# Layer 1 of a four-image kernel: TensorE's order made by an account of the engines instead of a fixed rate

## The chip, the cores and the metric

One core of a Trainium2 chip runs the whole program. The metric is the device time of one execution in microseconds (us). No die comparison is possible with one core; every run quoted here is of the undisturbed state ("fast"), and where single executions scatter, the granted TensorE clock of the record is given beside them.

## The reference, cut to what matters

Input x is 4 x 256 x 48 x 48, float32. Layer 0 is a normalised 3x3 convolution followed by attention over 2304 positions; layer 1 computes 45 guidance channels, turns them into weights by softmax, sums nine weighted shifts of the image for each of five dilations, and mixes the six results with a 1x1 convolution.

```python
def _L1_conv_ref(x, W_cat, W_scale, gamma, beta):          # cut
    guidance = _conv(x, W_cat, pad=1)                       # 45 channels
    outs = [x]
    for i, d in enumerate((1, 6, 12, 24, 36)):
        w = softmax(guidance[:, 9*i:9*(i+1)], axis=1)
        outs.append(_dyn_branch(x, w, d))                   # sum of 9 shifted, weighted copies
    y = _conv(concatenate(outs, axis=1), W_scale, pad=0)
    ...                                                     # batch normalisation over all images
# x = x + layer0(group_norm(x)); x = x + layer1(group_norm(x))
```

## The kernel before

Layer 1 of an image goes in six chunks of 384 positions. For each shift (a "tap") TensorE broadcasts the tap's weights over the partitions with one matmul into PSUM (`wb`), VectorE multiplies them with the shifted image (`prod`, or `cat` for the first tap of a dilation), and GpSimd adds the product to `cat`. When a dilation is complete, TensorE mixes it into `py` with four matmuls. Names of tiles in the profiles: the guidance goes `pg`, `lg`, `pt` (transposed), `e` (softmax), `pw` (transposed back), `w` (the weights); the convolution goes `pc`, then `cs` and `yt` (output transform), `hid`; `pq` and `pv` are the q, k and v products, `se` and `p` the scores and exponentials of the attention. In the trace of this kernel TensorE starts nothing of what stands behind a waiting matmul in its order: before the `pw` at 732.25 us, which waits for `w`, it stands 7.24 us without a matmul, and the filler behind it starts only at 732.94 us. So the program has to put other TensorE work between the `wb` matmuls: mixes that are due, steps of the next guidance (`ahead`), and the next image's convolution and q, k, v products (`other`, the filler). Before, a constant rate per element decides how much:

```python
            rate = (max(left, 0.0) + GUIDE * (NCK // 2 - 1) * 2 / NCK + mixes) / TAP_ELEMENTS
            ...
            def pump():
                nonlocal owed
                while owed > 0:
                    if queue and queue[0][0] <= tap:            # a mix, due so many taps later
                        owed -= queue.pop(0)[1]()
                        continue
                    if pace[1] < pace[0]:                       # a step of the next guidance
                        ...
                    got = next(other, None)                     # filler
                    ...
                    owed -= got
            ...
                    single = alone and at > 0 and j >= 10 and j % 5 == 0
                    ...                                         # wb matmul, product
                    if single:
                        ...                                     # TensorE mixes this product itself
                    elif at:
                        nc.gpsimd.tensor_tensor(dst, dst, pv, ALU.add)
                    tap += 1
                    owed += NH * nr * ncol * rate
                    pump()
            ...
            run(1e9)                                            # what is left of the filler
            for _, go in queue:                                 # then the last mixes
                go()
```

`alone` is the last image, which has no filler; there some taps are "single": TensorE mixes the product and GpSimd has no add. The convolution that serves as filler ends in an output transform on VectorE. Four of its instructions per unit (an image has four units) read two operands from SBUF (`d34` with `d12`, `s34` with `s12`):

```python
                elif i == 4:
                    tt(s34, m, first[at], ALU.add)              # m is in PSUM
                    tt(d34, first[at], m, ALU.subtract)
                elif i == 0:
                    result(1, d34, -2.0, d12)                   # yt <- cs, cs: both in SBUF
                    result(2, s34, -4.0, s12)
                    tt(s12, s12, s34, ALU.subtract)
                    axpy(d12, d34, -8.0, d12)
                    result(0, m, None, s12)
```

## Time and profile before

In profile lines PE is TensorE, PEld its weight loads, DVE VectorE, ACT ScalarE, POOL GpSimd and SPq a DMA queue; `a<-b` names what is written and what is read, and L with a number is a line of the kernel.

| | before |
|---|---|
| time, median of 3 runs | 3043.45 us (3041.85 to 3043.84) |
| span of the profiled execution | 3038.6 us |
| GpSimd's adds in the first layer-1 stage | 192, 258.6 us |
| TensorE's waits in it (six kinds) | 26.0 us |
| granted clock of TensorE, 545 to 868, 1262 to 1594 and 1985 to 2322 us | 0.98, 0.97, 0.97 |
| the same, 644.5 to 647.9, 709.3 to 712.7 and 729.8 to 736.6 us (13.6 us of the first stage) | 0.50, 0.51, 0.50 |
| the same, 720 to 740 us, which hold the 7.24 us wait of `pw` | 0.83 |
| first `wb` of the stage to the first exponential of the next attention | 301.9, 302.1, 302.1 us |

The prediction below shows the page, the groups and the waits of this kernel. Two more readings of it turn out to matter. First, the two `yt<-cs` groups of VectorE in the table of groups: in the window 545 to 868 us (the first layer-1 stage, with GpSimd adding) and in the window 0 to 140 us (the first image's own convolution, with GpSimd idle). The number after the comma is the mean of one instruction in ns.

```profile
L755 DVE SCALAR_TENSOR_TENSOR yt<-cs 128x288 f32<-128x288 f32 x8 | 9.3, 1199 | 0.0
...
L755 DVE SCALAR_TENSOR_TENSOR yt<-cs 128x288 f32<-128x288 f32 x8 | 3.3, 448 | 0.3 <-ACT hid L742 0.3
```

The same eight instructions on the same shapes take 1199 ns beside GpSimd's adds and 448 ns without them. The prediction used 1.2 us as if it were the work of the instruction.

Second, the end of the first stage in the timeline (start, duration, engine, and in brackets the idle time before it and what ended it): the last mixes, the copy of y, its store, and the first exponential of the attention that follows.

```profile
860.92 5.41 PE L1189 MATMUL py<-cat,wsc 128*128 128x384 f32 x16
...
866.41 0.80 ACT L1207 COPY y<-py 128x768 f32<-128x768 f32 x1 [4.84 <-PE py L1189]
867.23 0.51 SPq L1211 DMA_DIRECT2D y_d<-y  x1
...
870.52 3.77 ACT L906 ACTIVATE p<-se 128x1024 f32<-128x1024 f32 x4 [3.32 <-DMA y_d<-y]
```

The exponentials wait 3.3 us for the store of y, and TensorE, which has issued its first scores, waits behind them.

### The profile page before, as it was taken

What the parts mean: (1) busy time and instruction counts of PE and PEld (TensorE: products, weight loads), DVE (VectorE), ACT (ScalarE), POOL (GpSimd) and SP (SyncE); (2) the same over time, 40 slices, a digit from 0 to 9 for tenths busy, and PEclk for the clock granted to TensorE, in tenths of its full rate; (3) what the DMA queues carried; (4) which work ended last, traced back from release to release, by engine and by line L of the source; (5) the groups of instructions that cost most, each with busy time, mean ns of one, the idle gap of its engine ahead of it and who ended that gap; (6) DMA issues with size and microseconds to landing.
All of it is one profiled execution on the core that took longest, in us unless ns stands there. A gap on an engine that the chain in (4) does not pass through costs nothing. (4 is left out here: it accounts for less than half of the span.)

```text
span 3038.6 us, 43039 instructions
## 1 busy us (share of the span) xinstructions
PE 2836.5 (93%) x17526; PEld 1312.7 (43%) x17526; DVE 2425.0 (80%) x2312; ACT 1549.2 (51%) x1812; POOL 1107.0 (36%) x833
## 2 busy tenths in 40 slices
PE   7999999998999999998899999999899999987984
PEld 5622224565642222565662222346564222244653
DVE  6399999578869999777868999967776999976776
ACT  3489888101258888500218988820124888850003
POOL 1000000997930000488880000079794000006884
PEclk9999999999999999999999999999999999998997
DMA  4400000011030000010003000000002000022004
GB/s 175 94 1 6 6 11 7 27 36 34 19 79 6 6 1 11 22 42 24 29 6 79 6 6 11 6 27 27 21 6 42 6 1 6 11 88 90 1 1 178
DMA packets 77966, 95.54 MB, mean 31 GB/s; under 512 B 52144, under 2 KB 66752, under 8 KB 75968
## 3 DMA queue, kind: packets, MB, share of 16 engines
q1 hardware_dynamic: 76960, 87.31, 10.0%
q0 software_dynamic: 800, 5.41, 0.5%
q8 instruction: 139, 2.28, 0.3%
q14 instruction: 67, 0.55, 0.1%
HBM read 62.03 MB, written 30.67 MB: 31 GB/s over the span
## 5 line engine op out<-in xcount | busy, mean ns | idle before, releaser
L906 ACT ACTIVATE p<-se 128x1024 f32<-128x1024 f32 x1296 | 1259.3, 1026 | 252.2 <-PE se L897 215.9
L944 DVE TENSOR_TENSOR acc<-acc,p 128x2048 f32<-128x2048 f32 x536 | 1227.9, 2291 | 75.7 <-ACT p L906 29.5
L1280 POOL TENSOR_TENSOR cat<-cat,prod 128x752 f32<-128x752 f32 (+7 forms) x734 | 992.6, 1361 | 570.3 <-DVE prod L1267 529.5
L897 PE MATMUL se<-q,k 32*128 32x512 f32 (+1 forms) x5760 | 805.4, 593 | 12.4 <-ACT p L906 7.5
L1267 DVE TENSOR_TENSOR prod<-wb,pad 128x768 f32<-128x768 f32 (+7 forms) x768 | 552.5, 747 | 203.5 <-PE wb L1243 165.2
L927 PE MATMUL num<-p,vT 128*32 128x512 f32 (+1 forms) x5760 | 694.8, 562 | 8.6 <-ACT scratch L949 7.4
L897 PEld LDWEIGHTS se<-q,k 32*128 32x128 f32 x5760 | 292.6, 183 | 529.5 <-issue 307.9
L714 POOL TENSOR_TENSOR cv_q<-pad,cv_q 128x600 f32<-128x600 f32 x3 | 4.1, 1354 | 1317.3 <-ACT cv_q L712 1317.3
L1243 PE MATMUL wb<-w,pick 128*128 128x384 f32 (+3 forms) x888 | 434.3, 524 | 21.9 <-DVE prod L1267 21.3
L1189 PE MATMUL py<-cat,wsc 128*128 128x384 f32 x960 | 364.8, 506 | 29.0 <-POOL cat L1280 28.9
L927 PEld LDWEIGHTS num<-p,vT 128*32 128x32 f32 x5760 | 121.8, 108 | 487.5 <-issue 439.8
L1189 PEld LDWEIGHTS py<-cat,wsc 128*128 128x128 f32 x960 | 182.9, 197 | 126.3 <-POOL cat L1280 36.2
L1243 PEld LDWEIGHTS wb<-w,pick 128*128 128x128 f32 x888 | 167.1, 193 | 140.0 <-DVE prod L1267 43.4
L810 PE MATMUL pc<-cv_q,u 128*128 128x288 f32 x576 | 168.2, 424 | 6.3 <-DVE cv_q L716 6.3
L810 PE MATMUL pc<-cv_k,u 128*128 128x288 f32 x576 | 159.3, 406 | 1.4 <-ACT m L767 1.2
L1067 PE MATMUL pg<-pad,wcat 128*45 128x384 f32 x864 | 153.7, 499 | 2.4 <-DVE pad L589 1.5
L1260 DVE TENSOR_TENSOR cat<-wb,pad 128x768 f32<-128x768 f32 x120 | 114.2, 952 | 41.6 <-PE wb L1243 41.4
L742 ACT ACTIVATE hid<-yt,bn_t_f,bn_s 128x288 f32<-128x288 f32 x64 | 39.4, 625 | 199.6 <-DVE yt L755 114.1
L838 PE MATMUL pq<-hid,wqkv 128*128 128x384 f32 x384 | 135.7, 485 | 0.0
L810 PEld LDWEIGHTS pc<-cv_q,u 128*128 128x128 f32 x576 | 110.7, 199 | 32.6 <-DVE cv_q L716 6.3
L810 PEld LDWEIGHTS pc<-cv_k,u 128*128 128x128 f32 x576 | 105.8, 189 | 27.8 <-issue 1.8
L944 DVE TENSOR_TENSOR acc<-p,p 128x2048 f32<-128x2048 f32 x36 | 82.5, 2292 | 41.8 <-ACT p L906 41.8
(209 smaller groups left out, 1631.2 us busy)
## 6 DMA issues: line engine op xcount, KB each, us to landing
pad<-in_x SPq DMA_DIRECT2D x14, 1152.0 KB, 14.9
u<-u_d SPq DMA_DIRECT2D x18, 768.0 KB, 4.3
x_d<-pad SPq DMA_DIRECT2D x48, 192.0 KB, 2.5
xst<-in_x SPq DMA_DIRECT2D x36, 192.0 KB, 2.4
y_d<-y SPq DMA_DIRECT2D x18, 384.0 KB, 2.7
u_d<-u SPq DMA_DIRECT2D x6, 768.0 KB, 3.8
y<-y_d SPq DMA_DIRECT2D x2, 2304.0 KB, 14.2
x<-x_d SPq DMA_DIRECT2D x2, 2304.0 KB, 21.5
```

Of the source, the lines that this page charges most:

```text
L810: nc.tensor.matmul(m, u[:, h, kx, o * P : (o + 1) * P], halves[g][:, h, i, :, kx : kx + WW], start=(h == 0 and kx == 0), stop=(h == NH - 1 ...
L838: nc.tensor.matmul(pq[:, :CH], wqkv[:, i, s, g * P : (g + 1) * P], hid[:, i, cols], start=(i == 0), stop=(i == NH - 1),)
L897: nc.tensor.matmul(ss[j // 2][:, j % 2, at : at + n], k_[r, g, m * P : (m + 1) * P], q[r, g, q0 : q0 + n], start=True, stop=True,)
L906: nc.scalar.activation(p[:, 2 * pair : 2 * pair + 2, :], ss[pair], AF.Exp, scale=QS)
L927: nc.tensor.matmul(st["num"][r, at : at + n], vT[:, m, g * P + j * D : g * P + (j + 1) * D], p[:, j, at : at + n], start=(m == 0 and not s ...
L944: nc.vector.tensor_tensor(st["acc"], other, p, ALU.add)
L1067: nc.tensor.matmul(pg[64 * s : 64 * s + NG, :CH], wcat[:, i, k, :], window(gn, i, (c + s) * R, k // 3 - 1, k % 3 - 1), start=(i == 0 and k ...
L1189: nc.tensor.matmul(to, wsc[:, n * NH + i, o * P : (o + 1) * P], rhs(i), start=(n == 0 and i == 0), stop=(last and i == NH - 1),)
L1243: nc.tensor.matmul(pw[:, : nr * WW], pick[:, k : k + 1].to_broadcast([P, P]), w[:, l0 * WW : l1 * WW], start=True, stop=True,)
L1260: nc.vector.tensor_tensor(catv, wb, src, ALU.mult)
L1267: nc.vector.tensor_tensor(pv, wb, src, ALU.mult)
L1280: nc.gpsimd.tensor_tensor(dst, dst, pv, ALU.add)
```

## The change

Its intent: give TensorE other work exactly as long as the next `wb` would have to wait for its buffer. The program keeps, while it is being built, an account of when each engine is expected to be done (`Clock`), with a fixed duration for each instruction. Other work is issued until TensorE's account reaches the time at which the buffer comes free; a mix goes out when its addend is expected to be ready. In the last image a tap is single when GpSimd's account is further behind than TensorE's by `BEHIND`. At the end of a stage the queued mixes now come first and the rest of the filler last. A check of a flag in the last image also moves one chunk later.

```diff
+        class Clock:
+            def __call__(self, engine, ns, *after):
+                self.t[engine] = max(self.t[engine], *(a + 150.0 for a in after), 0.0) + ns
+                return self.t[engine]
...
                     else:
                         axpy(t, x, a, y)
+                        end = clock("DVE", 1200)
... (some thirty such entries)
-            def pump():
-                nonlocal owed
-                while owed > 0:
-                    if queue and queue[0][0] <= tap:
-                        owed -= queue.pop(0)[1]()
+            def fill(until):
+                while clock.t["PE"] < until:
+                    if queue and when(queue[0]) <= clock.t["PE"]:
+                        queue.pop(0)[-1]()
                         continue
... (then guidance steps, then filler, as before)
+                    fill(slot("wb", 5 if alone else 3))
                     pw = ps_w.tile([P, 512], F32, tag="w", name=f"wb_{b}_{c}_{k}")
...
-                    single = alone and at > 0 and j >= 10 and j % 5 == 0
+                    single = (
+                        alone and at > 0
+                        and clock.t["POOL"] + added > clock.t["PE"] + len(queue) * NH * MM + BEHIND
+                    )
...
+            while queue:
+                fill(when(queue[0]))
+                if queue:
+                    queue.pop(0)[-1]()
             ...
             run(1e9)
-            for _, go in queue:
-                go()
```

More of the change, by code (lines that the diff above doesn't have):

```diff
@@ L38 @@
 PRODS = 5
+BEHIND = 4000.0
 CONV_B, BN_G, BN_B, BN_M, BN_V, Q_B, K_B, PROJ_B, G1, B1 = range(10)
@@ L636, in conv_preact_kernel, with __init__, level, slot @@
         MM = 27.0 / 16 * CH
+        class Clock:
+            def __init__(self):
+                self.t = dict.fromkeys(("PE", "DVE", "ACT", "POOL"), 0.0)
+            def __call__(self, engine, ns, *after):
+                self.t[engine] = max(self.t[engine], *(a + 150.0 for a in after), 0.0) + ns
+                return self.t[engine]
+            def level(self):
+                self.t = dict.fromkeys(self.t, max(self.t.values()))
+        clock = Clock()
+        free = {}
+        def slot(tag, bufs):
+            ends = free.setdefault(tag, [])
+            return ends[-bufs] if len(ends) >= bufs else 0.0
         ORDER = (1, 2, 3, 4, 0, 5)
@@ L760, in result @@
                         tt(t, x, y, ALU.add)
+                        end = clock("DVE", 450, clock.t["PE"])
                     else:
                         axpy(t, x, a, y)
+                        end = clock("DVE", 1200)
                     relu(g, o, r, t)
+                    clock("ACT", 630, end)
+                    return end
                 if i in (1, 3):
@@ L767, in outputs @@
                     nc.scalar.copy(first[at], m)
+                    end = clock("ACT", 400, clock.t["PE"])
                 elif i == 2:
@@ L770, in outputs @@
                     tt(d12, first[at], m, ALU.subtract)
+                    end = clock("DVE", 900, clock.t["PE"])
                 elif i == 4:
@@ L773, in outputs @@
                     tt(d34, first[at], m, ALU.subtract)
+                    end = clock("DVE", 900, clock.t["PE"])
                 elif i == 0:
@@ L778, in outputs @@
                     axpy(d12, d34, -8.0, d12)
-                    result(0, m, None, s12)
-                else:
-                    result(3, m, None, d12)
+                    clock("DVE", 1400)
+                    end = result(0, m, None, s12)
+                else:
+                    end = result(3, m, None, d12)
+                free["c"].append(end)
             if b == 0:
@@ L807, in conv @@
                         m = pc[:, :TN]
+                        clock("PE", 0, slot("c", 2))
                         for h in range(NH):
@@ L816, in conv @@
                                 )
+                                clock("PE", MM * TN / CH)
                                 if h < NH - 1 or kx < 2:
@@ L836, in conv_qkv @@
                         pq = psum_tile(f"pq_{b}_{c}_{g}_{s}")
+                        end = clock("PE", 2 * MM, slot("c", 2))
                         for i in range(NH):
@@ L847, in conv_qkv @@
                         )
+                        free["c"].append(clock("ACT", 580, end))
+                        clock("DVE", 550, clock.t["ACT"])
                         nc.vector.tensor_reduce(
@@ L864, in conv_qkv @@
                 nc.scalar.copy(vT[:, t : t + 2, :], pv)
+                end = clock("PE", 4 * MM * C / CH, slot("c", 2))
+                free["c"].append(clock("ACT", 590, end))
                 if t == 0:
@@ L874, in conv_preact_kernel @@
         qkv = {}
-        CONV_QKV = MM * (6 * 4 * 6 * TN / CH + NCK * NH * 4 + NT * 2 * C / CH)
         def attention(b, q, k_, vT, pools, spare, project, scratch):
@@ L1074, in weights @@
                         if k % 3 == 2:
+                            clock("PE", 3 * MM)
                             yield 3 * MM
@@ L1077, in weights @@
                 nc.vector.tensor_copy(lg[64 : 64 + NG, :], pg[64 : 64 + NG, :CH])
+                clock("ACT", 480, clock.t["PE"])
+                clock("DVE", 560, clock.t["PE"])
                 yield -300.0
@@ L1095, in weights @@
                 nc.vector.tensor_reduce(mx, lt, AX.X, ALU.max)
+                clock("PE", 600)
+                clock("DVE", 430, clock.t["PE"])
                 yield -600.0
                 nc.vector.tensor_tensor(ek, lt, each(mx), ALU.subtract)
+                clock("DVE", 430)
                 yield -600.0
@@ L1102, in weights @@
                 nc.vector.tensor_reduce(sm, ek, AX.X, ALU.add)
+                clock("DVE", 430)
                 yield -600.0
                 nc.vector.reciprocal(sm, sm)
+                clock("DVE", 330)
                 yield -600.0
@@ L1107, in weights @@
                 nc.vector.tensor_tensor(ek, ek, each(sm), ALU.mult)
+                clock("DVE", 1800)
                 for _ in range(3):
@@ L1125, in weights @@
                     out.append(w)
+                    clock("PE", 600)
+                    clock("ACT", 480, clock.t["PE"])
+                    clock("DVE", 560, clock.t["ACT"])
                     yield -500.0
@@ L1131, in dynamic_filters @@
             ready = {}
-            GUIDE = 2 * NCK // 2 * 9 * MM
             while chunk < NCK:
@@ L1151, in dynamic_filters, with when, waiting, mixed @@
                     run(-got)
-            mixes = NCK * (1 + len(DILATIONS)) * NH * NH * MM
-            left = (CONV_QKV - spent[0] - 9000.0) if other is not None else 0.0
-            rate = (max(left, 0.0) + GUIDE * (NCK // 2 - 1) * 2 / NCK + mixes) / TAP_ELEMENTS
             queue = []
-            tap = 0
-            owed = 0.0
             ahead = iter(())
-            def pump():
-                nonlocal owed
-                while owed > 0:
-                    if queue and queue[0][0] <= tap:
-                        owed -= queue.pop(0)[1]()
-                        continue
-                    if pace[1] < pace[0]:
-                        got = next(ahead, None)
-                        if got is not None:
-                            pace[1] += 1
-                            owed -= max(got, 0.0)
-                            continue
-                    got = next(other, None)
-                    if got is None:
-                        owed = 0.0
-                        return
-                    owed -= got
+            def when(entry):
+                return entry[0] if entry[1] else slot("y", 1) + 150
+            def fill(until):
+                while clock.t["PE"] < until:
+                    if queue and when(queue[0]) <= clock.t["PE"]:
+                        queue.pop(0)[-1]()
+                        continue
+                    if pace[1] < pace[0] and next(ahead, None) is not None:
+                        pace[1] += 1
+                        continue
+                    if next(other, None) is None:
+                        return
+            def waiting(kind):
+                return sum(entry[1] == kind for entry in queue)
+            def mixed(kind, most):
+                while waiting(kind) > most:
+                    fill(when(queue[0]))
+                    if queue:
+                        queue.pop(0)[-1]()
             def mix(c, n, o, rhs, last=False, at=None):
@@ L1195, in go @@
                         )
+                    part = 1.0 if at is None else (l1 - l0) * (x1 - x0) / CH
+                    clock("PE", NH * MM * part, slot("y", 1) if n == 0 and o == 0 else 0.0)
                     if last and o == NH - 1:
                         done(c)
-                    return NH * MM
                 return go
@@ L1207, in done @@
                 nc.scalar.copy(yc, py.pop(c)[:, :, :CH])
+                free["y"].append(clock("ACT", 800, clock.t["PE"]))
+                clock("DVE", 1100, free["y"][-1])
                 for o in range(NH):
@@ L1215, in dynamic_filters @@
             STEPS = 24.0
+            clock.level()
+            free.update((tag, []) for tag in ("wb", "prod", "y"))
             for c in range(NCK):
@@ L1218, in dynamic_filters @@
                     back()
+                if alone and c == 2:
                     flag_of(misc("pf")[:1, : B * NH])
@@ L1224, in dynamic_filters @@
                     queue.append(
-                        (
-                            tap + (9 if alone else 14),
-                            mix(c, 0, o, lambda i, c=c: window(gn, i, c * R, 0, 0)),
-                        )
+                        (0.0, "", mix(c, 0, o, lambda i, c=c: window(gn, i, c * R, 0, 0)))
                     )
@@ L1235, in dynamic_filters @@
                     if at == 0:
+                        mixed("cat", NH * (CATS - 1))
                         cat = work1.tile(
@@ L1256, in dynamic_filters @@
                     src = gn[:, :, 1 + y0 + oy : 1 + y1 + oy, 1 + x0 + ox : 1 + x1 + ox]
-                    single = alone and at > 0 and j >= 10 and j % 5 == 0
+                    clock("PE", 0.45 * nr * WW + 20, slot("wb", 5 if alone else 3))
+                    ns = NH * nr * ncol
+                    ns, added = 1.05 * ns + 150, 2.1 * ns + (190 if ncol == WW else 80)
+                    single = (
+                        alone and at > 0
+                        and clock.t["POOL"] + added > clock.t["PE"] + len(queue) * NH * MM + BEHIND
+                    )
                     if at == 0:
                         nc.vector.tensor_tensor(catv, wb, src, ALU.mult)
+                        end = summed = clock("DVE", ns, clock.t["PE"])
                     else:
+                        if single:
+                            mixed("single", 2 * NH)
                         tag, bufs = ("single", 3) if single else ("prod", PRODS)
@@ L1267, in dynamic_filters @@
                         nc.vector.tensor_tensor(pv, wb, src, ALU.mult)
+                        end = clock(
+                            "DVE", ns, clock.t["PE"], 0.0 if single else slot("prod", PRODS)
+                        )
+                    free["wb"].append(end)
                     if single:
@@ L1270, in dynamic_filters @@
                             queue.append((
-                                tap + 6,
+                                end + 150, "single",
                                 mix(
@@ L1280, in dynamic_filters @@
                         nc.gpsimd.tensor_tensor(dst, dst, pv, ALU.add)
-                    tap += 1
-                    owed += NH * nr * ncol * rate
+                        summed = clock("POOL", added, end)
+                        free["prod"].append(summed)
                     pace[0] += STEPS * 1.15 * NH * nr * ncol * NCK / 2 / TAP_ELEMENTS
-                    pump()
                     if j + 1 == len(taps) or taps[j + 1][0] != n:
                         for o in range(NH):
-                            queue.append(
-                                (
-                                    tap + PRODS + 1,
-                                    mix(
-                                        c, n + 1, o, lambda i, cat=cat: cat[:, i, :],
-                                        n == len(DILATIONS) - 1,
-                                    ),
-                                )
-                            )
+                            queue.append((
+                                summed + 150, "cat",
+                                mix(
+                                    c, n + 1, o, lambda i, cat=cat: cat[:, i, :],
+                                    n == len(DILATIONS) - 1,
+                                ),
+                            ))
                 if c % 2 == 1:
@@ L1298, in dynamic_filters @@
                         pass
+            while queue:
+                fill(when(queue[0]))
+                if queue:
+                    queue.pop(0)[-1]()
             if alone:
```

## The prediction

> **What bounds the kernel now.** I read the page first (busy shares and the 40 slices), then the groups, the waits and the timeline of single stretches. The program takes four images in turn, each an attention stage and then a layer-1 stage; layer 1 of images 0 to 2 carries the convolution of the next image along as filler for TensorE, the last image has no filler.
>
> ```profile
> PE 2836.5 (93%) x17526; PEld 1312.7 (43%) x17526; DVE 2425.0 (80%) x2312; ACT 1549.2 (51%) x1812; POOL 1107.0 (36%) x833
> PE   7999999998999999998899999999899999987984
> POOL 1000000997930000488880000079794000006884
> ```
>
> GpSimd works in layer 1 alone: 545 to 868, 1262 to 1594, 1985 to 2322 and 2712 to 3004 us, some 1280 us in all. The change rearranges nothing outside these; the attention stages (about 1610 us) stay. The groups of image 0's layer 1, 545 to 868 us:
>
> ```profile
> L1280 POOL TENSOR_TENSOR cat<-cat,prod 128x768 f32<-128x768 f32 (+9 forms) x192 | 258.6, 1356 | 34.9 <-DVE prod L1267 24.0 <-POOL cat L1280 0.3
> L1267 DVE TENSOR_TENSOR prod<-wb,pad 128x768 f32<-128x768 f32 (+9 forms) x192 | 138.7, 746 | 48.1 <-PE wb L1243 36.4 <-POOL cat L1280 10.8
> ```
>
> GpSimd's 192 adds take 258.6 us, and stand between 572.6 and 861.8 us (289 us): it is 89% busy. To compare, I count TensorE's stream[...]. In the timeline a group of four py records (two matmuls of 384 columns) and one wb repeat every 1.47 us, so a matmul is 0.64 us and a wb 0.19. From the first wb on the stage issues py 144 x 0.64 = 92, wb 41, conv and q, k, v about 105, guidance 23, small ones 4: some 263 us in 301. So both are near full, and **GpSimd is the tighter one**. The waits of the same stage:
>
> ```profile
> PE pw L1114 <- DVE w L1122: 7.4, 2, 7.2
> PE py L1189 <- POOL cat L1280: 7.3, 6, 2.7
> PE wb L1243 <- DVE prod L1267: 7.1, 8, 3.0
> POOL cat L1280 <- DVE prod L1267: 24.0, 14, 4.2
> ```
>
> TensorE waits some 25 us per stage, but what ends the stage is GpSimd, and its reachable loss is the 24.0 us it waits for products; the other 10.9 of 34.9 us are about 55 ns at each of 192 adds and stay. Fourteen of the 24 us lie between 690 and 745 us. There:
>
> ```profile
> 695.49 3.06 DVE L755 SCALAR_TENSOR_TENSOR yt<-cs 128x288 f32<-128x288 f32 x2
> 700.58 7.53 POOL L1280 TENSOR_TENSOR cat<-cat,prod 128x576 f32<-128x576 f32 x5 [2.35 <-DVE prod L1267]
> ...
> 704.68 2.58 DVE L755 SCALAR_TENSOR_TENSOR yt<-cs 128x288 f32<-128x288 f32 x2
> ```
>
> VectorE, not TensorE, is overfull: the convolution's four result units (from the table of groups, two of 1.2 us, one of 0.96, two of 0.45 each, some 4.3 us per unit) stand in front of the products.
>
> In the last image (158 adds, 216.4 us) GpSimd waits 457.3 - 435.7 = 21.6 us for products. The longest piece is the chain that makes the tap weights, with nothing beside it:
>
> ```profile
> 2887.24 2.14 PE L1067 MATMUL pg<-pad,wcat 128*45 128x384 f32 x12
> ...
> 2895.27 0.88 PE L1114 MATMUL pw<-ident,e 128*128 128x128 f32 x3 [3.36 <-DVE e L1107]
> ...
> 2900.35 3.06 POOL L1280 TENSOR_TENSOR cat<-cat,prod 128x672 f32<-128x672 f32 x2 [7.17 <-DVE prod L1267]
> ```
>
> [...]1005 ns for 384 elements, 1820 for 768, a slope of 2.12 ns. The new account uses 2.1 ns plus 80 or 190, so its GpSimd is right to about 1% (1803 against 1820; 1659 against 1653 for 752 elements). Its VectorE (1.05 ns plus 150: 956 against 950) is right too. [...]the 7.2 us wait of pw held all filler behind it. [...]the 20 us that hold this wait show a granted clock of 0.83.
>
> **The change part by part.** I compared the built orders; counts of work are unchanged in images 0 to 2.
>
> (a) *The account instead of a rate, images 0 to 2.* Before each wb, TensorE is given other work only until the wb's buffer is expected free. In the built order the work ahead of the 60th wb falls from 68 to 61 us, of the 120th from 138 to 134, of the 216th from 245 to 239; the adds up to there need 73, 144 and 256. So products run ahead of GpSimd more, and the waits outside the crowded stretch (24.0 - 14.0 = 10 us) should shrink to about 3, the 1 to 2 us of the start among them: gain 7.
>
> (b) *The crowded stretch.* The new order still feeds the four result units within about 14 taps. There VectorE needs 4 x 4.3 = 17 for the units, 4 for statistics and weights, 13 for the products: 34 us. GpSimd needs 20 us for those adds and holds at most five products, about 7 us. It must idle about 34 - 20 - 7 = 7 us where it lost 14. Gain 7, the least certain term.
>
> (c) *The end of the stage.* Before, all v matmuls were issued before the last mixes. Now four pv groups (4 x 1.7 = 6.8 us) stand after them. In the old trace the last mixes streamed until 866.4 and the next exponentials waited until 870.5 for the store of y; that is 8.7 us after the last add. In the new order it is 2.6 (last mix) + 6.8 + 1.5 = 10.9, but the store is then hidden. Loss 2.
>
> Per image 7 + 7 - 2 = 12; I take 11, since three timings must hold together. Three images: 33 us.
>
> (d) *The last image.* Singles fall from 34 to 25 but become larger ones. By the per-form durations GpSimd's adds rise from 218 to 222 us, TensorE's single mixes fall from 58 to 54: nearly no transfer of load. Against that, the account has less reason to fill, so the guidance steps lag: the built order now has two bare chains. After the last wb of chunk 1 come two guidance steps, the transposes and both pw before the first wb of chunk 2; the same at chunk 3 to 4 with one step. From the old trace, last pg to next wb is 2889.4 to 2897.9, 8.5 us. With 3.9 us of pg ahead and 2.3 us to the first new add, less about 4 us of held products, GpSimd idles some 10.7 us; for the second chain 1.9 + 8.5 + 2.3 - 3.5 = 9. Two chains cost 20 where one cost 7.2. The remaining 14 us of waits should fall to about 6. Net: 4 + 13 - 8 = 9 us longer; I take 8, as the account might use the pause.
>
> Sum: -33 + 8 = -25 us, 3043 - 25 = **3018 us**.
>
> **The rivals.** *TensorE is the bound, and its waits (25 to 28 us per stage, plus some 7 us of slow clock) all come back.* For it: 93% busy and a busy map of nines. Against: streaming only 263 of 301 us, and GpSimd's 258.6 us of adds with 10.9 us of gaps start at 572.6, so they cannot end before 842. Even with every wait gone this gives 20 us per image: about 2980 with a neutral last image. *The bare chains dominate.* If both cost 15 us and the crowded stretch does not improve, the sum is 3 x -4 + 18: about 3050. *The account is off at each step because it doesn't know the statistics and normalisation of VectorE (12 x 0.55 us per stage)*, so wb matmuls wait for buffers in order[...]. Then the gain of (a) vanishes and (c) stays: about 3043 to 3055. The durations agree so well that I give this little weight.
>
> **Range and chances.** Terms (a) and (b) together may be 4 to 19 us per image, (d) may be -6 to +20: 3018 less 32 at best and plus 25 otherwise. Range 2986 to 3043. Over 2% faster means below 2982.6, which needs nearly all of GpSimd's waits back in all four images: 0.08. Over 2% slower (above 3104) would need a stall that I don't see in the order: 0.02. Within 2%: 0.90.
>
> **What would show it.** (a): GpSimd's wait for products per stage falls from 24 to about 10 us, adds still 258.6. (b): what remains sits where VectorE runs the STT results. (c): pv matmuls after the last py, and no wait of the exponentials for y's store. (d): in the last image two GpSimd waits of 8 to 11 us, each behind the weights' chain, and about 167 adds of 222 us. The prediction is wrong if adds themselves get longer, if the wait of wb for products grows, or if the two chains are covered.

## The result, and the profile after

The changed kernel took 3027.09 us (median of 4 runs, 3026.57 to 3028.31) against 3043.44 us (median of 4, 3041.85 to 3043.84) of the kernel before. The ratio is 0.9948, 95% interval 0.9931 to 0.9965: the same within 2%, and 16 us faster. Ratios here are the mean time of one kernel's fast runs over that of the other's in the same rounds, so they are not quite the ratio of the medians quoted.

The page of the changed kernel, the same two rows that the prediction shows of before:

```profile
PE 2834.9 (94%) x17454; PEld 1303.8 (43%) x17454; DVE 2419.1 (80%) x2312; ACT 1549.8 (51%) x1812; POOL 1109.4 (37%) x842
...
POOL 1000000898930000389880000078894000007884
```

Busy shares say nothing about the 16 us. The groups of GpSimd in the first stage and its wait, and the waits of TensorE there (total us, times, longest):

```profile
L1349 POOL TENSOR_TENSOR cat<-cat,prod 128x768 f32<-128x768 f32 (+9 forms) x192 | 258.2, 1355 | 29.1 <-DVE prod L1332 18.3
```

```profile
PE pt L1124 <- DVE lg L1117: 6.8, 2, 3.5
PE pw L1162 <- DVE e L1154: 6.2, 2, 6.0
PE pc L844 <- DVE yt L784: 4.2, 2, 2.4
PE pq L874 <- DVE yt L784: 2.0, 1, 2.0
PE wb L1299 <- DVE prod L1332: 1.5, 5, 0.6
PE pw L1162 <- DVE w L1170: 1.2, 2, 1.0
PE py L1240 <- POOL cat L1349: 1.0, 2, 0.7
```

The three waits that led before (pw for w 7.4, py for cat 7.3, wb for prod 7.1) have shrunk to 1.2, 1.0 and 1.5 us: the account does what it was built for. But pt for lg, pw for e, and pc and pq for yt have grown from 3.3 us together to 19.2. The sum is 22.9 us where it was 25.1 for the same kinds. All the new waits stand behind VectorE. The `e` that pw waits for is one of the instructions that run long beside GpSimd, and the `yt` that pc and pq wait for, 0.45 us of work itself, stands behind two more of them in VectorE's order. `lg` is none of them:

```profile
L779 DVE SCALAR_TENSOR_TENSOR yt<-cs 128x288 f32<-128x288 f32 x8 | 9.8, 1259 | 0.0
L1154 DVE TENSOR_TENSOR e<-e,sm 128x270 f32<-128x270 f32 x3 | 4.4, 1478 | 0.1
L1153 DVE TENSOR_TENSOR e<-e,sm 128x270 f32<-128x270 f32 x3 | 3.6, 1194 | 0.0
```

The end of the first stage in the timeline of the changed kernel: the rest of the filler (pv) stands after the last mixes, the store of y lies beside it, and the exponentials wait only for their scores.

```profile
859.83 7.07 PE L895 MATMUL pv<-wqkv,hid 128*128 128x256 f32 x32
860.07 0.80 ACT L1259 COPY y<-py 128x768 f32<-128x768 f32 x1 [2.04 <-PE py L1240]
860.89 0.52 SPq L1265 DMA_DIRECT2D y_d<-y  x1
...
868.87 3.77 ACT L945 ACTIVATE p<-se 128x1024 f32<-128x1024 f32 x4 [1.35 <-PE se L936]
```

The last image, GpSimd's timeline: two long pauses for products and one of 0.3 us, where the kernel before had sixteen that add up to 21.6 us.

```profile
2822.09 12.16 POOL L1349 TENSOR_TENSOR cat<-cat,prod 128x752 f32<-128x752 f32 x7 [9.34 <-DVE prod L1332]
2834.59 67.39 POOL L1349 TENSOR_TENSOR cat<-cat,prod 128x672 f32<-128x672 f32 x46 [0.34 <-DVE prod L1332]
2908.39 75.98 POOL L1349 TENSOR_TENSOR cat<-cat,prod 128x752 f32<-128x752 f32 x57 [6.41 <-DVE prod L1332]
```

Where the 13.8 us between the two profiled spans lie, read from the first `wb` matmul of each stage and the first exponential after it (us; the two right columns are runs explained below):

| stretch | before | changed | changed, run again | changed, old end order |
|---|---|---|---|---|
| start to first `wb` of image 0 | 568.6 | 570.0 | 568.2 | 572.1 |
| layer 1 of image 0, to the first exponential | 301.9 | 298.9 | 301.6 | 301.3 |
| attention of image 1 | 424.9 | 423.8 | 423.8 | 422.4 |
| layer 1 of image 1 | 302.1 | 302.7 | 300.2 | 301.5 |
| attention of image 2 | 424.9 | 422.0 | 423.5 | 424.9 |
| layer 1 of image 2 | 302.1 | 301.2 | 299.9 | 304.3 |
| attention of image 3 | 419.7 | 416.9 | 416.6 | 421.5 |
| layer 1 of image 3 and the end | 294.3 | 289.3 | 289.3 | 289.2 |
| span | 3038.6 | 3024.8 | 3023.0 | 3037.2 |

The three middle layer-1 stages, from which the prediction wanted 33 us, gave 3.4 us together; the stretches after them 6.8, the last image 5.0, and the start cost 1.4. Single stretches differ by up to 2.7 us between two executions of the same kernel, so only the sums are used.

### The profile page after: what moved, and what is told of

Same layout as the page of the kernel before. It is cut to its first block, busy times and chain, and to the rows that moved or that the text cites. A ratio compares the mean times of both kernels' runs of the same rounds, so it can differ in the third digit from the quotient of the medians.

```text
span 3024.8 us, 42936 instructions
## 1 busy us (share of the span) xinstructions
PE 2834.9 (94%) x17454; PEld 1303.8 (43%) x17454; DVE 2419.1 (80%) x2312; ACT 1549.8 (51%) x1812; POOL 1109.4 (37%) x842
## 5 line engine op out<-in xcount | busy, mean ns | idle before, releaser
L738 POOL TENSOR_TENSOR cv_q<-pad,cv_q 128x600 f32<-128x600 f32 x3 | 4.1, 1353 | 1322.5 <-ACT cv_q L736 1322.5
L1299 PE MATMUL wb<-w,pick 128*128 128x384 f32 (+3 forms) x888 | 395.5, 495 | 11.7 <-DVE prod L1332 10.0
L1240 PE MATMUL py<-cat,wsc 128*128 128x384 f32 x960 | 354.9, 497 | 5.5 <-POOL cat L1349 5.3
```

The costliest lines, as they stand in the source:

```text
L1240: nc.tensor.matmul(to, wsc[:, n * NH + i, o * P : (o + 1) * P], rhs(i), start=(n == 0 and i == 0), stop=(last and i == NH - 1),)
L1299: nc.tensor.matmul(pw[:, : nr * WW], pick[:, k : k + 1].to_broadcast([P, P]), w[:, l0 * WW : l1 * WW], start=True, stop=True,)
```

## The experiments

Twelve runs were made: ten edits, one of them twice, and the changed kernel once more. Each was compared with the kernel before in the same rounds; "+" and "-" are against the changed kernel unless said otherwise.

### Who ends a stage?

```diff
+                        twice = 2 if b > 0 and g == 0 else 1
...                                                     # the account's entry, times twice
-                        for i in range(NH):
+                        for i in list(range(NH)) * twice:
```

> The changed kernel with 12 q and k groups issued twice in each convolution that runs under the adds: 12 x 1.28 = 15.4 us more of TensorE's stream in each of three stages, 46 us in all, none of it waiting for GpSimd; the result is unchanged. Theory 1 (TensorE's stream and waits end the stage, GpSimd has slack at its end): about 3027 + 46 = 3073, between 3064 and 3078. Rival (GpSimd ends the stage, as I predicted): TensorE fills its own waits with the extra work, and the time rises by less than 25 us.

Measured: 3071.89 us (3070.51 to 3074.39), ratio 1.0101 (1.0087 to 1.0116). That is 45 us over the changed kernel, for 46 us of added TensorE work. GpSimd's waits hardly moved (18.2 us in the first stage against 18.3). In the timeline of the first stage, GpSimd's last adds and TensorE's last filler:

```profile
744.18 112.15 POOL L1350 TENSOR_TENSOR cat<-cat,prod 128x672 f32<-128x672 f32 x83 [2.46 <-DVE prod L1333]
865.80 15.70 PE L896 MATMUL pv<-wqkv,hid 128*128 128x256 f32 x72
```

GpSimd is done at 856.3 us (857.0 without the added work), TensorE's filler only at 881.5 (866.9). Almost every microsecond given to TensorE lengthens the program, so **TensorE's stream ends these stages of the changed kernel, not GpSimd**. Two limits belong to this. The account puts nearly all of the added work behind the last mixes, so the run could hardly have filled earlier waits with it. And it was not run on the kernel before, of which my premise spoke. There the trace has to do: its last mixes stream without a break from 860.92 to 866.33 us, so they do not wait for GpSimd's last add, which ends at 861.8. The premise is refuted for the changed kernel, and read from the trace for the one before.

### Is a late VectorE instruction an instruction blocked by GpSimd?

The four two-SBUF-operand instructions of the output transform read the PSUM tile `m` in place of `d34` or `s34`. The values are wrong on purpose.

```diff
-                    result(1, d34, -2.0, d12)
-                    result(2, s34, -4.0, s12)
-                    tt(s12, s12, s34, ALU.subtract)
-                    axpy(d12, d34, -8.0, d12)
+                    result(1, m, -2.0, d12)
+                    result(2, m, -4.0, s12)
+                    tt(s12, s12, m, ALU.subtract)
+                    axpy(d12, m, -8.0, d12)
```

> The changed kernel with a result that is wrong on purpose: in the four result units of the convolution, the two scaled adds into yt, the update of s12 and the update of d12 read the matmul's PSUM tile where they read d34 or s34 from SBUF. Count, shape and place of the instructions stay. Theory 1 (a VectorE instruction with two SBUF operands waits for GpSimd's running add): the yt ones fall from 1.26 us under the adds to about 0.45, as in the stretch without adds; TensorE's waits for yt (6.2 us per stage) go to under 1 us; GpSimd's waits for products between 700 and 750 us fall from 12 us to under 5; the time falls by 6 to 8 us in each of three stages, to 3003 to 3010. Rival (VectorE simply has too many instructions in that stretch, as I predicted): the yt ones stay at 1.2 us or the time stays within 5 us of 3027.

Measured: 11777.75 us, because the wrong values tripped the kernel's own safety check and the slow general path ran afterwards (which is also why the output was right). The total is of no use; the four layer-1 stages ran before that and can be read in the trace. Groups of VectorE, and waits of TensorE and GpSimd in the first stage:

```profile
L779 DVE SCALAR_TENSOR_TENSOR yt<-pc,cs 128x288 f32<-128x288 f32 x8 | 3.3, 448 | 0.0
```

```profile
PE pc L844 <- DVE yt L784: 0.7, 1, 0.7
```

```profile
POOL cat L1349 <- DVE prod L1332: 14.6, 9, 3.9
```

With one operand in PSUM the instruction takes 448 ns beside the adds, as it takes without them: so 0.81 us of its 1259 ns were waiting. How it waits can be read from single instructions. An add and a `yt` of the changed kernel, from the timeline of 731.7 to 733.0 us:

```profile
731.79 1.49 POOL L1349 TENSOR_TENSOR cat<-cat,prod 128x672 f32<-128x672 f32 x1 [2.39 <-DVE prod L1332]
732.50 1.10 DVE L779 SCALAR_TENSOR_TENSOR yt<-cs 128x288 f32<-128x288 f32 x1
```

The add ends at 733.28 us, the `yt` 0.32 us later. In the layer-1 stages of the kernel before and of the changed one, 62 instructions of VectorE with two SBUF operands took over 0.55 us, and each of them ended 0.30 to 0.32 us after the end of an add. With no add running, such instructions took 0.44 to 0.46 us. So a long one waits until the running add has ended. The adds themselves are hardly longer: 1355 ns on average in the first stage of the changed kernel, 1353 in that of the run with both regroupings (below); one that follows directly on the add that a long instruction waited for took 0.06 to 0.2 us more than others of its shape. Not all four per unit are long: in the first stage of the changed kernel the updates of `s12` and `d12`, with GpSimd idle after the second `yt`, take 458 and 452 ns.

TensorE's wait for yt falls from 4.2 to 0.7 us (its 2.0 us at pq stays, so that under 1 us in all was a miss). GpSimd's waits in the three stages fall from 18.3, 22.0, 18.9 to 14.6, 13.4, 15.3, those between 700 and 750 us from 12.0 to 6.0, not under 5: what is left of the crowded stretch is not the `yt`. From the first `wb` of image 0 to that of image 3 the trace shows 2148.3 us against 2165.5: 17 us less, just under the 6 to 8 us per stage expected, for the eight `yt` per image freed.

### The last image: the bare chains and the rule for singles

First, the steps of the next weights are forced to their pace in the last image, so that no chain stands bare:

```diff
+                    while alone and pace[1] < pace[0]:
+                        if next(ahead, None) is None:
+                            break
+                        pace[1] += 1
```

> The changed kernel where, in the last image alone, the guidance and weight steps are issued when their pace says, before filling, and not only when a fill has nothing else. Theory (the two bare chains at the end of chunks 1 and 3 cost the GpSimd 9.3 and 6.4 us): both waits go, the last image is 12 to 16 us shorter, the time 3011 to 3016. Rival (GpSimd's work simply moves to later waits, or TensorE is the bound there too): less than 6 us gained, 3021 or more.

Measured: 3026.26 us (3025.09 to 3028.62), ratio 0.9952 (0.9939 to 0.9965), against 0.9948 of the changed kernel: no gain. The timeline of GpSimd in the last image:

```profile
2741.43 77.69 POOL L1353 TENSOR_TENSOR cat<-cat,prod 128x658 f32<-128x658 f32 x59 [435.60 <-DVE prod L1336]
2823.38 159.53 POOL L1353 TENSOR_TENSOR cat<-cat,prod 128x752 f32<-128x752 f32 x113 [4.26 <-DVE prod L1336]
```

The pauses of 9.3 and 6.4 us are gone, and only 4.3 us is left, but the rule made fewer taps single: 172 adds of 227.7 us in place of 167 of 220.1. With the first add also 3.7 us later after the first `wb` (the forced steps stand in front), the 11.8 us of pauses were spent again. The expected 12 to 16 us did not come.

Second, the old rule for singles with the new order:

```diff
-                    single = (
-                        alone and at > 0
-                        and clock.t["POOL"] + added > clock.t["PE"] + len(queue) * NH * MM + BEHIND
-                    )
+                    single = alone and at > 0 and j >= 10 and j % 5 == 0
```

> The changed kernel's order by account, with the old fixed rule for single mixes in the last image (34 singles, GpSimd's adds 218 us by the per-form durations where they are 222). If the new rule for singles gives what the last image gained: 5 to 12 us slower than the changed kernel, 3032 to 3039. If the account gives it and the rule is neutral: within 4 us of 3027. If the new rule's heavier load of GpSimd costs: 3018 to 3023.

Measured: 3029.79 us (3026.1 to 3031.54), ratio 0.9959 (0.9946 to 0.9971). The medians put the new rule at about 3 us; the intervals overlap, so it may be worth nothing. This is the case of a neutral rule.

### The blocked instructions taken away, with correct results

The output transform regrouped so that each VectorE instruction has at most one SBUF operand; the results are correct.

```diff
-                elif i == 0:
-                    result(1, d34, -2.0, d12)
-                    ...
+                elif i == 3:                         # m in PSUM is the first operand everywhere
+                    stt_psum(d34, -2.0, d12)
+                    stt_psum(s34, -4.0, s12)
+                    stt_psum(s12, -1.0, s12)
+                    stt_psum(d12, -8.0, d12)
+                elif i == 4:
+                    shown(1, 2.0, d34)
+                    shown(2, -4.0, s34)
+                    stt_psum(s12, -1.0, s12)
+                    stt_psum(d12, 8.0, d12)
...                                                  # i == 0 keeps result(0, m, None, s12) alone
```

Not shown: ScalarE's copy of product 3 is no longer needed, and the account's entries follow the new order.

> The changed kernel with the convolution's output transform regrouped so that each VectorE instruction reads one operand from PSUM and one from SBUF: the sums with products 3 and 4 are added straight from their PSUM tiles in units 3 and 4; the result is right, 12 instead of 10 VectorE instructions per group and none with two SBUF operands. Theory 1 (exclusion by GpSimd's adds, and TensorE's stream with its waits ends the stage): no result instruction over 0.5 us, TensorE's 4 us waits of pc for yt go, 5 to 7 us less in each of three stages as in the wrong-on-purpose run, time 3006 to 3013. Rival (VectorE overfull by count): no gain, as it has two instructions more; 3022 or more.

Measured: 3012.4 us (3011.39 to 3015.52), ratio 0.9903 (0.9886 to 0.9919), some 14 us under the changed kernel (which ran in other rounds; by the ratios 0.0045 of 3042 us), although it has 32 VectorE instructions more. The regrouping also moves instructions to earlier products and drops the copy, so alone it would not separate the blocking. But from the first `wb` of image 0 to that of image 3 it takes 2146.3 us against 2165.5, 19 us less where the operand swap, which moved nothing, gave 17; the first stage began 5 us later.

Then the softmax too: the exponentials are written to PSUM, so that the two multiplications read one SBUF operand.

```diff
-                nc.scalar.activation(ek, ek, AF.Exp)
+                nc.scalar.activation(lt, ek, AF.Exp)      # lt is in PSUM
...                                                   # the sum reads lt too
-                nc.vector.tensor_tensor(ek2, ek, each(sm), ALU.mult)
+                nc.vector.tensor_tensor(ek2, lt, each(sm), ALU.mult)
...                                                   # the second product likewise; the account's entry 1800 becomes 900
```

> The run before, and the softmax of the tap weights keeps its exponentials in PSUM, so that its sum and its two products read one operand from PSUM. Theory 1: TensorE's wait of pw for e (6 us once per stage) falls under 2 us, the two products from up to 1.9 to about 0.45 us; 3 to 5 us less per stage and 1 to 4 in the last image: 10 to 18 us below the run before, 2990 to 3002. Rival (pw waits because the products stand before e in VectorE's queue, whatever their operands): within 4 us of the run before.

Measured: 3002.83 us (3002.14 to 3003.16), ratio 0.9868 (0.9852 to 0.9885), 10 us below the run before. The two multiplications in the groups of VectorE, and what TensorE and GpSimd still wait for in the first stage:

```profile
L1166 DVE TENSOR_TENSOR e<-pt,sm 128x270 f32<-128x270 f32 x3 | 1.3, 433 | 0.0
L1167 DVE TENSOR_TENSOR e<-pt,sm 128x270 f32<-128x270 f32 x3 | 1.3, 429 | 0.0
```

```profile
PE pt L1137 <- DVE lg L1130: 7.6, 2, 4.3
PE pw L1175 <- DVE e L1167: 4.0, 1, 4.0
```

```profile
POOL cat L1362 <- DVE prod L1345: 12.0, 12, 3.2
```

The instructions are at 0.43 us where they were at 1.19 and 1.48 in the changed kernel and 0.75 and 1.48 in the run before, and no wait for yt is left among TensorE's waits. But the wait for e, which was to fall under 2 us, is still 4.0 (5.8 in the run before), and that for lg 7.6. So of the 19.2 us of new waits 11.6 are not the blocking; those I did not take apart.

Last of this group, both regroupings in the kernel *before*, with its constant rate, its singles and its end order (one check of a flag moved a chunk later, as the changed kernel has it):

> The kernel before, in its old order, with both of these regroupings (and its flag check one chunk later, so that the PSUM tile is free). If the blocked VectorE instructions were what hid the account's gain, the account is worth more without them: this run stays 25 us or more above the run with both in the new order. If the waits that both orders meet are simply those instructions and the account's worth is separate: 12 to 20 us above it. If the old order's losses were mostly these instructions: less than 8 us above it. My guess is the second: 3008 to 3018.

Measured: 3006.09 us (3003.25 to 3010.35), ratio 0.988 (0.9863 to 0.9896). Without a line of the account it is 36.5 us under the kernel before, and 3.3 us over the changed kernel with the same regroupings. My guess, 12 to 20 us, was wrong; the third case came, in which the old order's losses were mostly these instructions. With the blocked instructions the whole change is worth 16 us, without them 3. Since no account is in this kernel, better entries in the account are not what the regroupings gain by. Up to the first exponential, its three middle stages take 290.5, 290.3 and 290.2 us, the waits for the store of y (3.15 to 3.35 us each) included, where those of the changed kernel with the same regroupings take 292.7, 289.3 and 292.9. So in the stages themselves the account shows no gain here; the attention stretches after them are 7.6 us shorter together with the changed order.

### The order at the end of a stage

The changed kernel with the filler before the queued mixes again, as in the kernel before:

```diff
+            if not alone:
+                run(1e9)
             while queue:
                 fill(when(queue[0]))
```

> The changed kernel with the end of each stage in the order of the kernel before: the other filler (the P times V products) first, then the queued mixes. The theory that TensorE's stream ends the stage expects no gain from the moved mixes themselves, since the tail is TensorE work without a wait in either order: within 3 us of 3027, or up to 9 us slower where the store of y is no longer hidden behind the products. My prediction's part (c) counted a loss of about 2 us a stage for the order of the changed kernel, so that undoing it would give about 3021.

Measured: 3033.47 us, but its 14 executions scatter from 3026.97 to 3045.09; ratio 0.9979 (0.9968 to 0.9991). So it was repeated beside the unedited changed kernel:

> The changed kernel itself, unedited, to be compared with w2_filler_first_again on one chip and in the same rounds, since z2_filler_first scattered over 18 us and was set against a run of the changed kernel from another day's rounds. Expected: 3027 again, 14 to 16 us below the kernel before.

> The same kernel as z2_filler_first (changed kernel, end of each stage in the old order). If the hidden store of y is what the new end order gains, this is 5 to 10 us slower than w1_after_again, 3 us for each of three stages. If z2_filler_first's difference came from its scatter, the two agree within 3 us. My prediction's part (c) says it is 6 us faster.

Measured in the same rounds: the changed kernel 3026.61 us (5 runs, 3024.86 to 3027.49; ratio 0.9947, 0.9934 to 0.996), the old end order 3039.05 us (22 runs, 3028.59 to 3047.8; ratio 0.9984, 0.9975 to 0.9994). The medians lie 12.4 us apart, the fastest runs 3.7. The first exponential of the second attention in the timeline of the old end order:

```profile
869.27 0.80 ACT L1259 COPY y<-py 128x768 f32<-128x768 f32 x1 [4.84 <-PE py L1240]
873.40 3.77 ACT L945 ACTIVATE p<-se 128x1024 f32<-128x1024 f32 x4 [3.33 <-DMA y_d<-y]
```

The wait for the store of y is back, at each of the three stages (3.3, 3.5 and 3.2 us). **My part (c), a loss of 2 us a stage, has the wrong sign**: the new end order gains, between 4 and 12 us in all. The size is uncertain because the executions of this one kernel scatter together with their granted clock: the 22 runs go from 3028.6 us at 0.980 to 3047.8 us at 0.973. In the two profiled executions, the 20 us from 860, 1590 and 2310 on show a clock of 1.00, 0.91 and 0.93 with the old end order and 1.00 each time with the new one, so some of the lost clock lies where TensorE waits behind the store. But 3.9 us of the difference between the two profiles is already there at the first `wb`, before the edit does anything. Why the clock varies between these executions, and hardly between the 5 of the changed kernel in the same rounds (0.977 to 0.978), stays open. Read the other way, this run is the account with the old end order: 3.5 us under the kernel before by the medians of these rounds (8.0 in the rounds of its first run). In the table its three middle stages take 907 us together, those of the kernel before 906, and its last image is 5 us shorter. So no gain of the account in the middle stages shows.

### The versions that the experiments point to

Both regroupings, the paced weights in the last image after its first taps, and a lower threshold for singles:

```diff
-BEHIND = 4000.0
+BEHIND = -2000.0
...
+                    while alone and (c > 0 or j > 6) and pace[1] < pace[0]:
```

> Both regroupings in the new order, and in the last image the weight steps on their pace after the first eight taps, with the threshold for single mixes at -2 us for 4, so that about five taps more are mixed singly than with the pace alone. Theory (in the paced run the two waits of GpSimd went, but five more adds, 7.6 us, and a start 3.7 us later took the gain): GpSimd's adds about 219 us in the last image, its span from first to last add 232 to 236 where the changed kernel had 245.5; 8 to 12 us below the run with both regroupings, 2980 to 2993. Rival (TensorE then ends the last image): within 4 us of it.

Measured: 2998.45 us (2997.32 to 2999.44), ratio 0.9856 (0.9839 to 0.9872). The last image and the end take 282.7 us (289.3 in the changed kernel), with 167 adds as there and 10.0 us of pauses against 16.1. Expected were 8 to 12 us below the run with both regroupings; the total is 4.4 below, as the first stage began 3.8 us later. In all four kernels with the regrouped transform, the first stage began late, in this one at 578.4 us. There, with GpSimd idle, the regrouping has nothing to free and adds two instructions per unit (0.45 us each, as long as the old ones). So the first image's convolution got its old transform back (a branch on `b == 0`):

> As y4_best, but the first image's own convolution keeps the old output transform. In all four kernels with the regrouped transform, the first stage began 4 to 6 us later (first write-back matmul 574.5 to 578.4 us against 570.0), because the convolution in the clear, with GpSimd idle, gains nothing from a PSUM operand[...]. Expected: the first stage begins at about 570 us and the total is about 5 us below y4_best, 2991 to 2996. If it stays within 2 us of y4_best, the later start has another cause.

Measured: 2990.35 us (2987.14 to 2992.4), ratio 0.9833 (0.9821 to 0.9846). The first stage begins at 565.9 us, and the total is 8 us under the version before it (in other rounds; 7 by the ratios), a little more than I expected. Single executions of equal instructions put that beginning between 568.2 and 572.1 us, so a part of it may be scatter. This is the fastest version: 51 us under the kernel before in its rounds and some 36 us under the changed one. The page and GpSimd's wait in the first stage:

```profile
PE 2825.1 (95%) x17454; PEld 1296.0 (43%) x17454; DVE 2389.6 (80%) x2336; ACT 1542.9 (52%) x1800; POOL 1106.7 (37%) x842
```

```profile
POOL cat L1389 <- DVE prod L1372: 10.2, 12, 1.5
```

## Why the prediction was right or wrong

**The total** (3018 us predicted, 3027 measured, in the range and in the class) was right, by terms that were not: 33 us of gain in three images and 8 of loss in the last were forecast, and some 10 and 5 of gain came. The wrong ones partly cancelled each other, so its nearness is luck. None of the three signs of being wrong that I had named came (adds 258.2 us, wb for prod 1.5, both chains bare): they tested details, not the premise. The sign of (a), GpSimd's wait at 10 us, failed. Two sums are off as well: the parts of TensorE's stream add up to 265 us, not 263, and the worst ends of the terms (three images of 4 - 2 us gained, 20 lost in the last) to 3057 us, not 3043.

**"GpSimd is the tighter one."** Wrong. I compared TensorE's streaming (263 of 301 us, an estimate) with GpSimd's adds (89% busy) and took the fuller one for the bound. Adding work to TensorE cost 45 of 46 us. The 38 us that I left free on TensorE were not free: some 26 of them are waits for VectorE or GpSimd at fixed places of its order. An engine with 263 us of streaming and its waits in the chain ends the stage just as well. The first rival, that TensorE is the bound and its waits come back, was right about the bound; but its waits did not come back where they were, they moved, from 25.1 to 22.9 us in all.

**(a), 7 us per stage.** GpSimd's wait for products fell from 24.0 to 18.3 us in the first stage, to 22.0 and 18.9 in the others, not to about 10. What I said would shrink did in part, outside the crowded stretch of the first stage from 10.0 to 6.3 us (I said 3): after the crowded stretch GpSimd adds for 112 us in one piece without a pause. But since GpSimd does not end the stage, its 5 us earlier end hardly helps: TensorE still streams pv until 866.9.

**(b), 7 us per stage, called the least certain.** This is the step with the wrong mechanism. I took the convolution's result units as 4.3 us of VectorE work each and called VectorE "overfull". The two of 1.2 us are 0.45 us of work each, the rest waiting for GpSimd's adds; so is half of the one of 0.96. The loop is closed: VectorE waits for GpSimd's add, the products behind it are late, and GpSimd then waits for products. Freeing the `yt` took 4 to 9 us of GpSimd's 18 to 22 us of wait per stage; the crowded stretch of the first stage lost 12.0 us where I forecast 7, and still 6.0 with the `yt` freed. The operand swap shows the cause; the regrouped kernels show its size: some 14 us for the transform alone and another 10 us for the softmax. The trace of before showed it too, and I had it open: 1199 ns in one window and 448 in another, for one instruction on one shape. The account has the same blind spot. It charges 1200, 1400 and 1800 ns for these instructions at every place; in the first stage of the changed kernel they took 1259, 910 and 2672 on average (one `yt`, both updates, both products), in the last image the products took 972.

(a) and (b) were to give 14 us per stage; with (c) counted in, the measured stages gave 1.1 on average, and the stretch after them 2.3.

**(c), a loss of 2 us per stage.** Wrong in sign. I measured the end from GpSimd's last add and so counted the pv groups behind it as added delay. For TensorE, which has to do them in any case, they are what it does while y is copied and stored. The new order removes three waits of 3.3 us, and with them some slow clock (0.91 and 0.93 where 1.00 was measured with the new order, in the 20 us from 1590 and 2310 on). In its own rounds it makes between 4 and 12 of the 16 us that the change gains.

**(d), the last image 8 us longer.** It became 5.0 us shorter. The two bare chains are there as read from the order: 9.3 and 6.4 us for my 10.7 and 9. So are the 167 adds, 222.0 us by the sum of durations that I had used (220.1 us busy). Two terms were mis-sized. The remaining waits fell to 0.3 us, not to 6; and the first add follows the first `wb` by 3.4 us where it was 7.2, because a guidance step no longer stands in front of the second `wb`. The sum of the measured parts is adds (busy) +3.7, waits 16.1 - 21.6 = -5.5, start -3.8: -5.6 us. Both single experiments on this image say that neither the chains nor the rule is worth more than some 3 us by itself.

**What is shown and what is not.** Shown: TensorE's stream ends the middle stages of the changed kernel; the long VectorE instructions wait for the end of an add; freeing them gives 24 us on the changed kernel and 37 on the kernel before. Not isolated by an edit: the account alone, without the new end order, once nothing is blocked. The 3 us between the two regrouped kernels include the hidden store, and the stages show no gain beside it. Open too: the waits of pt for lg (7.6 us) and of pw for e (4.0 us) that remain in each stage.

## What to carry to other kernels

Before an order is tuned around the durations of a trace, compare each group's mean in a stretch where the neighbours are idle with its mean where they work: an instruction that takes 448 ns alone and 1259 beside GpSimd is a wait in disguise, and here removing it (one operand in PSUM) gained 24 us more, where the whole change of the order had gained 16. To learn which engine ends a stage, give it a known amount of extra work and look for it in the total; a busy share and a streaming sum did not decide it here (TensorE was busy for 93%, 94% and 95% of the span, its weight loads for 43% each time, at 3043, 3027 and 2990 us). At a stage's end, put work that must be done anyway behind the last result that has to be copied and stored: here three waits of 3.2 to 3.5 us went.
